# A quantised cross-attention with a gated LoRA layer: the order of four small products, and the queue of 32 stores

## The chip, the cores and the metric

The kernel runs on one core of one Trainium2 chip. A core has a tensor engine (PE; its weight loads are listed as PEld), a vector engine (DVE), a scalar engine (ACT), GpSimd (POOL) and SyncE (SP), which here only issues DMA transfers. The metric is the device time of one execution in microseconds, as the median of several runs.

## The reference

Two residual steps on x of shape 2 x 1024 x 2048, float32. The first adds a quantised product with a context of 2 x 2048 x 2048; the second adds a linear layer with one shared low-rank adapter and one that is a sum of sixteen, weighted by a gate. The 2 x 1024 rows form eight groups of 256, and each has its own row of the gate:

```python
q1 = fake_quant(_layernorm(x), x1_scale, x1_zp)     # clip(round(v / s + z), 0, 255), back to float
q2 = fake_quant(ctx_4096, x2_scale, x2_zp)
x = x + jnp.matmul(q1, q2)

h = _layernorm(x)
base_out = jnp.matmul(h, kernel) + bias
A_eff = jnp.einsum('bn,nri->bri', gate, lora_A)      # gate 8 x 16, lora_A 16 x 32 x 2048
B_eff = jnp.einsum('bn,nor->bor', gate, lora_B)      # lora_B 16 x 2048 x 32
h8 = h.reshape(8, 256, 2048)
Ax = jnp.einsum('bri,bti->btr', A_eff, h8)
delta = jnp.einsum('bor,btr->bto', B_eff, Ax)
delta = delta + jnp.einsum('or,btr->bto', lora_B_shared, jnp.einsum('ri,bti->btr', lora_A_shared, h8))
x = x + base_out + delta.reshape(x.shape)
```

## The kernel before

The function works through the two batches one after the other. All of it is written in a framework whose scheduler, before the kernel runs, puts the instructions of each engine into one fixed order; only the entry of batch 0 has an order written out by hand. Every engine takes its instructions in that order, and an instruction that waits holds up all that stand behind it on its engine. A `high_priority` block, and a change in the work around an instruction, move it in that order.

**Cross-attention.** For each batch, the product is cut into four blocks n of 512 columns and four groups g of 256 rows, each with two row tiles j. One pair (n, g) is `xattn_pair`: for each j, ACT fills PSUM with the row and column terms (`begin`, L526), PE adds 16 products in bf16 (tile pa, L530, 16 products of 128 x 512), then DVE adds both row tiles to x (`end`, L547) and takes statistics for the second layer norm (L551). The right operand comes from the context, which SP loads in 512 KB pieces into buffers of a pool called lit and ACT and DVE quantise.

**Gating.** The gated adapters are made by PE: for each batch four blocks of A and four blocks of B, each of 512 columns. For one such block `gated_sums` (L570) takes two loaded buffers of two halves each; each half, 128 x 512 (the sixteen adapters by eight of the 32 ranks), goes through one float32 product with a matrix of gate values (gmat) into 32 of the 128 rows of one PSUM bank (eight ranks for each of the batch's four groups; tile pg_a or pg_b, L576). So a block has four products, c = 0 to 3. Each buffer is given back after its two products, and the next load is issued by `load_next` (L204) on SP's queue, from one list `todo` that holds the context's pieces and the adapters' in the order of their use. `gated_copy` (L588) copies the bank to SBUF on DVE (L591, buffers of a pool q2b). A's blocks are turned by PE and placed into acat (L594 to L610). B's blocks go to a DRAM tensor bd: `lora_b_step` (L612) issues eight stores for each block, each of 16 rows of 512 float32, 32 KB, from SP (L617). From bd they come back as tiles bp (L680, loads of 64 rows), of which the first two of a batch are issued from POOL's queue and the others from ACT's.

**From cross-attention to the second layer.** When a group's 256 rows are finished, `group_z` normalises them: DVE works out the scale of each row tile from the statistics (L334 to L358) and scales it in two halves (z, L629), PE transposes each half in two sets (tile ptz, L633), ACT copies these to SBUF (L634), and ACT's queue stores the result to DRAM (zs, L640, four stores of 512 KB for each group). `lora_ax` multiplies two groups with acat (px, L649).

**Second layer.** The product with the weight is a Strassen-like scheme, twice nested. SP loads blocks of the weight of 1 MB (big<-in_w_dram, L753), DVE adds two of them (L763) into operands named b11, b12, b22, b21 and combines these (L772); POOL does the same for the operands made from z (a11, a21, a22, a12 and the sums s1, s2). PE multiplies (tiles fu, fv, fw, L829), DVE adds the results to y (L853), and the second adapter product (pl, L695) needs bp. The first operands of a batch, and first products fu, are prepared while its cross-attention still runs, and stand among its instructions.

Of the kernel before, what the change touches and what calls it, by code (L numbers as in the profile page):

```python
# [98 lines left out]
def tile_quant_xattn_then_lora_ffn(  # L99
# [17 lines left out]
    nc = tc.nc  # L117
# [15 lines left out]
    GP = GPB * RC  # L133
# [21 lines left out]
    gmat = const.tile([P, 2, GPB // 2, RC], F32, tag="gmat", name="gmat")  # L155
# [48 lines left out]
    def load_next():  # L204
        while todo and len(loaded) < ahead[0] and todo[0][0] <= batch[0] and lit.spare:
            _, srcs = todo.popleft()
            if isinstance(srcs, int):
                load_x(0, srcs)
                continue
            buf = lit.take()  # L210
            t = flat(buf).rearrange("p (k n) -> p k n", k=2)
            if len(srcs) == 1:
                nc.sync.dma_start(out=t, in_=srcs[0])
            else:
                for c, src in enumerate(srcs):
                    nc.sync.dma_start(out=t[:, c, :], in_=src)
            loaded.append((len(srcs), buf, t))

    def next_loaded(parts):

        got = next(e for e in loaded if e[0] == parts)
        loaded.remove(got)
        return got[1:]
# [342 lines left out]
    def gated(nm):  # L566

        return gated_copy(gated_sums(nm))

    def gated_sums(nm):  # L570
        ps = ps_m.tile([P, NB], F32, tag="pm", name=f"pg_{nm}")
        for h in range(2):
            buf, t = next_loaded(2)
            for c in range(2):
                row = (2 * h + c) * GP
                nc.tensor.matmul(  # L576
                    ps[row : row + GP, :],
                    gmat.rearrange("p i a r -> p (i a r)"),
                    t[:, c, :],
                    start=True,  # L580
                    stop=True,
                    skip_group_check=True,
                )
            lit.give(buf)
            load_next()
        return ps
# [25 lines left out]
    def lora_b_step(b, n):  # L612

        st, sf = gated(f"b{b}_{n}")
        for c in range(NC):
            for i in range(2):
                nc.sync.dma_start(  # L617
                    out=bd[b][i::2, i, ds(c * RC, RC), ds(n * NB, NB)],
                    in_=sf[ds(c * GP + i * (GP // 2), GP // 2), :],
                )  # L620
        q2b.give(st)
# [301 lines left out]
    def entry():  # L923
# [21 lines left out]
        def ad_sums(n):  # L945
            ad[n] = gated_sums(f"a0_{n}")
# [74 lines left out]
    for b in range(B):  # L1021
# [35 lines left out]
        for g in range(GPB):  # L1057
# [6 lines left out]
            if g == 2:  # L1064
                column_term(b, 3, c2[3])
        lora_b_step(b, 0)
        close_c2(2)
        bp.give(colt.pop(2))
# [3 lines left out]
        for g in range(GPB):  # L1072
            xattn_pair(b, 3, g, c1T, c2[3])
            big.give(c1T_bufs[g])
            if g == 0:
                first.block("b11")
                first.load("b12")
            elif g == 1:
                first.block("b12")
                first.comb("t1", "b12", "b11", ALU.subtract)  # L1080
            elif g == 2:
                first.load("b22")
            if g < 3:
                lora_b_step(b, g + 1)
            if g > 0:
                zqs[g - 1] = [lit.take() for _ in range(4)]
                group_z(b, g - 1, wk, zqs[g - 1])
            if g == 2:

                lora_ax(b, 0, [zqs[0], zqs[1]])  # L1090
                for i in range(2):
                    for j in range(2):
                        first.t[f"a{i + 1}{j + 1}"] = zqs[i][j]
                        lit.give(zqs[i][2 + j])
# [127 lines left out]
```

## Time and profile before

| what | value |
|---|---|
| median of three runs | 1090.15 us (1088.11 to 1092.04) |
| span of the profiled execution | 1086.6 us |
| PE busy | 1063.4 us in 3932 records |
| DVE busy | 759.3 us |
| POOL busy | 267.8 us |
| ACT busy | 247.6 us |
| granted clock of PE, mean | 0.994 |

The span runs from the first to the last instruction that the profiler saw in one execution; the time of a run also holds what lies around it, so it is some microseconds longer (3.5 us between this span and the median). Busy times are per engine, and engines work beside each other. In a row such as "L530 PE MATMUL pa<-big,big 128*128 128x512 bf16 x1024 | 238.8, 381 | 5.0 <-DVE big L428 2.6", the parts are: line, engine, operation, output and inputs, shape, number; then busy microseconds and the mean nanoseconds of one; then how long the engine sat idle just before such instructions and what ended most of that. A float32 product shows as two records. In timelines the columns are start, duration, engine, line, operation, tile, count, and in brackets an idle time ahead of it with what ended it. SPq and ACTq are the queues in which SP and ACT issue transfers.

### The profile page before, as it was taken

How to read it: one execution, taken by the hardware profiler on the slowest of the kernel's cores; microseconds unless marked ns; L12 is line 12 of the kernel's file. 1: busy time of each engine (PE TensorE's matmuls, PEld its weight loads, DVE VectorE, ACT ScalarE, POOL GpSimd, SP SyncE). 2: the span in 40 equal slices, each digit the busy share in tenths (PEclk: the TensorE clock that was granted, in tenths of full speed). 3: DMA queues.
4: the chain of work that ended last, by engine and by line, in shares of the span. 5: the costliest groups of instructions: out<-in, count | busy, mean ns of one | idle time of the engine just before them, and what ended most of it. 6: DMA issues, size and time to landing. Idle time of an engine off the chain costs nothing.

```text
span 1086.6 us, 10640 instructions
## 1 busy us (share of the span) xinstructions
PE 1063.4 (98%) x3932; PEld 491.3 (45%) x3932; DVE 759.3 (70%) x941; ACT 247.6 (23%) x351; POOL 267.8 (25%) x112
## 2 busy tenths in 40 slices
PE   5999999999999999999999999999999999999998
PEld 2444445544444444444444433555444444444443
DVE  7986776756877686677858645757569677756851
ACT  5866133210000000001676631331000000000000
POOL 0000003243434314362000000034344532253500
PEclk7999999999999999999999999999999999999999
DMA  9979758876897575798682394679668874748511
GB/s 344 378 200 295 214 189 327 311 250 218 290 361 271 181 269 182 255 357 300 221 281 49 124 245 164 222 273 349 237 237 292 293 266 154 270 144 301 212 40 58
DMA packets 120380, 261.35 MB, mean 241 GB/s; under 512 B 11400, under 2 KB 15624, under 8 KB 119304
## 3 DMA queue, kind: packets, MB, share of 16 engines
q1 hardware_dynamic: 99840, 219.24, 59.1%
q10 hardware_dynamic: 20168, 40.38, 10.9%
q0 software_dynamic: 320, 1.05, 0.3%
q8 instruction: 31, 0.51, 0.2%
q14 instruction: 21, 0.17, 0.1%
HBM read 224.99 MB, written 37.75 MB: 242 GB/s over the span
## 4 chain that ended last, share of the span: by engine, by line
PE 87%; DVE 5%; DMA 4%; ACT 2%; issue 1%; SPq 0%; ACTq 0%
PE fu L829 34%; PE fv L829 17%; PE pa L530 14%; PE fw L829 9%; DMA lit<-in_ctx_dram 3%; PE pl L695 3%; PE px L649 3%; PE ptz L633 2%; DMA y<-in_x_dram 1%; PE pg_b L576 1%; DVE st L383 1%; PE pg_a L576 1%; ACT big L412 1%; PE pt L423 1%; DVE big L629 1%
## 5 line engine op out<-in xcount | busy, mean ns | idle before, releaser
L829 PE MATMUL fu<-big,lit 128*128 128x512 f32 x896 | 395.3, 593 | 0.0
L829 PEld LDWEIGHTS fu<-big,lit 128*128 128x128 f32 x896 | 168.7, 190 | 206.2 <-issue 204.9
L530 PE MATMUL pa<-big,big 128*128 128x512 bf16 x1024 | 238.8, 381 | 5.0 <-DVE big L428 2.6
L829 PE MATMUL fv<-big,lit 128*128 128x512 f32 x448 | 197.9, 594 | 0.0
L772 POOL TENSOR_TENSOR lit<-lit,lit 128x1024 f32<-128x1024 f32 x56 | 164.2, 2940 | 116.4 <-PE fw L829 49.2
L763 POOL TENSOR_TENSOR lit<-lit,lit 128x1024 f32<-128x1024 f32 x40 | 100.2, 2508 | 289.1 <-DMA lit<-zs 257.7
L772 DVE TENSOR_TENSOR big<-big,big 128x2048 f32<-128x2048 f32 x56 | 159.6, 2853 | 5.9 <-PE ptz L633 5.3
L530 PEld LDWEIGHTS <-big 128*128 128x128 bf16 x1024 | 96.7, 98 | 136.5 <-issue 31.8
L853 DVE TENSOR_TENSOR y<-y,fu 128x1024 f32<-128x1024 f32 x92 | 108.6, 1215 | 50.7 <-PE fu L829 50.5
L829 PEld LDWEIGHTS fv<-big,lit 128*128 128x128 f32 x448 | 84.3, 190 | 105.0 <-issue 104.7
L853 DVE TENSOR_TENSOR y<-y,fv 128x1024 f32<-128x1024 f32 x48 | 56.8, 1218 | 89.4 <-PE fv L829 89.4
L458 ACT ACTIVATE q2b<-lit,sc,inv 128x1024 int16<-128x1024 f32 x64 | 76.3, 1232 | 161.8 <-DMA lit<-in_ctx_dram 126.1
L763 DVE TENSOR_TENSOR big<-big,big 128x2048 f32<-128x2048 f32 x40 | 104.2, 2604 | 11.8 <-DMA big<-in_w_dram 11.8
L829 PE MATMUL fw<-big,lit 128*128 128x512 f32 x224 | 99.6, 593 | 0.0
L680 POOL DMA_DIRECT2D bp<-bd x4 | 2.7, 664 | 376.8 <-DVE rstd_z L358 183.4
L684 ACT COPY pl<-bias 128x1024 f32<-128x1024 f32 x16 | 16.3, 1018 | 294.4 <-DVE y L706 281.4
L547 DVE SCALAR_TENSOR_TENSOR y<-pa,k_s,y 128x1024 f32<-128x1024 f32 x32 | 41.0, 1280 | 47.0 <-PE pa L530 46.8
L829 PEld LDWEIGHTS fw<-big,lit 128*128 128x128 f32 x224 | 41.8, 190 | 51.4 <-issue 50.2
L853 DVE TENSOR_TENSOR y<-y,fw 128x1024 f32<-128x1024 f32 x24 | 28.4, 1216 | 50.9 <-PE fw L829 50.9
L526 ACT ACTIVATE pa<-bp,r_s 128x512 f32<-128x512 f32 x58 | 39.0, 685 | 84.8 <-PE pa L530 54.8
L383 DVE BATCH_NORM_STATS2 st<-y 128x6 f32<-128x512 f32 x64 | 41.4, 680 | 5.4 <-DMA y<-in_x_dram 5.3
L551 DVE BATCH_NORM_STATS2 st<-y 128x6 f32<-128x512 f32 x64 | 40.1, 678 | 0.1
(92 smaller groups left out, 637.3 us busy)
## 6 DMA issues: line engine op xcount, KB each, us to landing
big<-in_w_dram SPq DMA_DIRECT2D x96, 1024.0 KB
lit<-zs SPq DMA_DIRECT2D x88, 512.0 KB
lit<-in_ctx_dram SPq DMA_DIRECT2D x64, 512.0 KB
out_dram<-y ACTq DMA_DIRECT2D x30, 512.0 KB
zs<-lit ACTq DMA_DIRECT2D x24, 512.0 KB
lit<-in_lora_a_dram SPq DMA_DIRECT2D x32, 256.0 KB
lit<-in_lora_bt_dram SPq DMA_DIRECT2D x32, 256.0 KB
y<-in_x_dram SPq DMA_DIRECT2D x16, 512.0 KB
```

The source lines that it names most:

```text
L383: nc.vector.bn_stats(st1[:, self.m, n, :], self.y[:, ds(n * NB, NB)])
L458: nc.scalar.activation(qi, t, AF.Relu, bias=z2, scale=inv2)
L526: nc.scalar.activation(self.pa[:, j, :], colt[self.n], AF.Identity, bias=r_s[:, m : m + 1])
L530: nc.tensor.matmul(self.pa[:, j, :], self.c1T[:, k, ds(j * P, P)], self.c2[k // 8][:, k % 8, :], start=not self.begun[j], stop=(k == KT - ...
L547: return nc.vector.scalar_tensor_tensor(yp, self.pa, s12, yp, ALU.mult, ALU.add)
L551: nc.vector.bn_stats(st2[:, self.g * MG + j, self.n, :], y[self.g][:, j, ds(self.n * NB, NB)])
L649: nc.tensor.matmul(px[i * 2 * R : (i + 1) * 2 * R, :], acat[:, k, ds(3 * pr + i, 2), :].rearrange("p s r -> p (s r)"), zqs[i][k // KQ][:, ...
L695: nc.tensor.matmul(pl[j][i][:, half], axT[rows, pr, ds(j * P, P)], bt[rows, half], start=False, stop=True, skip_group_check=True,)
L763: line(eng.tensor_tensor(got[0], got[0], got[1], ALU.add if terms[1][2] > 0 else ALU.subtract))
L772: line(eng.tensor_tensor(out_t, at[p], at[q], op))
L829: nc.tensor.matmul(ps[m], at[:, k, ds(m * P, P)], bt[:, k, :], start=(opens and k == 0), stop=(ends and k == KQ - 1), skip_group_check=True,)
L853: line(nc.vector.tensor_tensor(yp, yp, whole[chain], op))
```

## The change

`gated_sums` takes both loaded buffers first, issues its four products one after the other in the order c = 3, 2, 1, 0, and gives both buffers back after the fourth, with the two next loads issued then. `lora_b_step` issues its eight stores on GpSimd's queue in place of SP's. Nothing else is edited; the lines after L577 move up by one.

```diff
     def gated_sums(nm):
         ps = ps_m.tile([P, NB], F32, tag="pm", name=f"pg_{nm}")
-        for h in range(2):
-            buf, t = next_loaded(2)
-            for c in range(2):
-                row = (2 * h + c) * GP
-                nc.tensor.matmul(
-                    ps[row : row + GP, :],
-                    gmat.rearrange("p i a r -> p (i a r)"),
-                    t[:, c, :],
-                    start=True,
-                    stop=True,
-                    skip_group_check=True,
-                )
+        got = [next_loaded(2) for _ in range(2)]
+        for c in (3, 2, 1, 0):
+            nc.tensor.matmul(
+                ps[c * GP : (c + 1) * GP, :],
+                gmat.rearrange("p i a r -> p (i a r)"),
+                got[c // 2][1][:, c % 2, :],
+                start=True,
+                stop=True,
+                skip_group_check=True,
+            )
+        for buf, _ in got:
             lit.give(buf)
             load_next()
         return ps
...
         for c in range(NC):
             for i in range(2):
-                nc.sync.dma_start(
+                nc.gpsimd.dma_start(
                     out=bd[b][i::2, i, ds(c * RC, RC), ds(n * NB, NB)],
                     in_=sf[ds(c * GP + i * (GP // 2), GP // 2), :],
                 )
         q2b.give(st)
```

## Prediction

> **What bounds the kernel now.** I read the page's head and busy times first, then the summary of the chain of waits, then the groups by line of the two gating products, and last the timelines of the engines in the stretches that the change touches (80 to 215 us for batch 0, 605 to 745 us for batch 1).
>
> ```profile
> span 1086.6 us, 10640 instructions
> PE 1063.4 (98%) x3932; PEld 491.3 (45%) x3932; DVE 759.3 (70%) x941; ACT 247.6 (23%) x351; POOL 267.8 (25%) x112
> PE 87%; DVE 5%; DMA 4%; ACT 2%; issue 1%; SPq 0%; ACTq 0%
> ```
>
> PE is the bound: 1063.4 of 1086.6 us busy, so at most 23 us could be won by filling its gaps, and most of those lie at the two ends. A microsecond of work taken from PE's row is a microsecond won, as long as nothing else is late. The groups by line, with shapes apart, give the touched products:
>
> ```profile
> L576 PE MATMUL pg_b<-lit,gmat 128*32 128x512 f32 x64 | 13.7, 605 | 0.0
> L576 PE MATMUL pg_a<-lit,gmat 128*32 128x512 f32 x64 | 12.7, 605 | 0.0
> ```
>
> 128 records are 64 products (two each), 16 blocks of four. The busy times differ though the counts agree; the chain in order of time (start, duration, what) tells why:
>
> ```profile
> 128.31 1.00 PE pg_b L576 x8
> 129.30 3.56 PE pa L530 x16
> 132.86 0.98 PE pg_b L576 x2
> 133.84 3.56 PE pa L530 x16
> 137.40 0.99 PE pg_b L576 x6
> ...
> 158.70 0.99 PE pg_b L576 x8
> ```
>
> Four products that stand together hold PE for 1.00 us, three for 0.99, one alone for 0.98: each uses 32 of PE's columns, and by these times neighbours run beside each other. A block that is split in 1 + 3 by 16 products of the cross-attention (pa, 3.56 us) costs 0.98 + 0.99 where a whole one costs 1.00.
>
> **The change part by part.** *One row.* Of 16 blocks, 9 are split so in this trace: three in batch 0 (starts at 104.87, 132.86, 141.95) and six in batch 1 (608.89, 636.99, 646.51, 657.97, 667.05, 676.14). In the order of instructions that the compiler gives the changed kernel all 16 stand as four in a row, at the place of the former lone one. That removes 9 x 0.98 = 8.8 us of PE work, 2.9 in batch 0 and 5.9 in batch 1. Taking both buffers at once adds a wait for the second load, but the adapter loads land early: the closest, pg_a of block 2, has its data at about 95.7 us for a use at 104.8, and those of B stand 20 us ahead. I cost it at nothing. That c runs 3 to 0 costs nothing either: same four, same columns. If the second load came late, the price would be that delay, once.
>
> *The stores.* 32 per batch leave SP's queue for POOL's. On SP they stand between the loads of the weight blocks:
>
> ```profile
> 126.61 2.10 SPq L753 DMA_DIRECT2D big<-in_w_dram  x2
> 130.25 5.24 SPq L617 DMA_DIRECT2D bd<-q2b  x8
> 137.43 0.93 SPq L753 DMA_DIRECT2D big<-in_w_dram  x2
> 139.34 18.47 SPq L617 DMA_DIRECT2D bd<-q2b  x16
> 157.92 1.37 SPq L753 DMA_DIRECT2D big<-in_w_dram  x2
> 160.65 10.68 SPq L617 DMA_DIRECT2D bd<-q2b  x8
> ```
>
> Eight take 5.2 us there. POOL has nothing between 2 us and 162.87 and issues only two loads of the same buffer (bp<-bd) before its first sum:
>
> ```profile
> 162.87 1.01 POOL L680 DMA_DIRECT2D bp<-bd  x1 [160.87 <-DMA zs<-lit]
> 180.60 0.54 POOL L680 DMA_DIRECT2D bp<-bd  x1 [16.71 <-DVE big L629]
> 181.16 9.50 POOL L772 TENSOR_TENSOR lit<-lit,lit 128x1024 f32<-128x1024 f32 x3
> ```
>
> The four issues of this kind in the whole trace take 538 to 1013 ns and their data lands in 5.2 to 6.0 us. No store is issued from POOL in this trace, so 0.54 and 1.01 us are the bounds from the nearest rows: 17 to 32 us per batch, in at least 50 us of an idle engine (130.5, the first copy of B, to 181). What queues behind them there are the bp loads, first needed by PE at 199.1 us (pl, L695), and the sums s1, s2, needed by PE at about 208.5. Both have 15 us or more left, so I cost the issues at nothing; without that cover 32 x 0.66 us, the four rows' mean, would be 21 us a batch. The ninth store and later ones wait for a lane that an earlier store frees, and the copy of the fourth B block waits for the first eight stores; at 6 us to landing these are done long before.
>
> The row that speaks against it is the 1013 ns issue, which stands beside the scaling of z on DVE (L629), where those beside other work of DVE took 0.54 to 0.56 us. The Trainium skill ("SBUF — State Buffer", section "SBUF: two separate sides") says that GpSimd writes the descriptors itself and is kept from it while DVE holds the port they share, 620 ns alone and 3100 beside a DVE copy; by that figure 32 stores would be an estimated 99 us a batch at the worst, and the sum would turn to a loss.
>
> *What moves on DVE.* This is the costly side. Without stores before them, SP's weight loads are expected earlier, and the compiler places DVE's weight sums (L763) earlier in DVE's order too: b12 now ahead of the end of pa_3_1 (L547) and of z_1 (L629), b22 ahead of the statistics and z_2, b21 ahead of z_5. PE's transposes ptz wait for z. DVE takes its queue in order, so each of these is a wait for a load with z behind it. In the old order:
>
> ```profile
> 146.52 1.28 DVE L547 SCALAR_TENSOR_TENSOR y<-pa,k_s,y 128x1024 f32<-128x1024 f32 x1 [3.00 <-PE pa L530]
> ...
> 149.51 2.27 DVE L763 TENSOR_TENSOR big<-big,big 128x2048 f32<-128x2048 f32 x1
> 151.70 0.81 DVE L629 TENSOR_SCALAR big<-y,mv_z,rstd_z 128x1024 f32<-128x1024 f32 x1
> ...
> 169.50 2.29 DVE L763 TENSOR_TENSOR big<-big,big 128x2048 f32<-128x2048 f32 x1 [1.01 <-DMA big<-in_w_dram]
> ```
>
> b12: its loads can issue at about 136.4 (pg's old 137.40 less the lone 0.98); those issued at 126.61 and 128.34 let DVE begin at 135.00, 8.4 to 8.9 us after the first. So L763 runs 145.3 to 147.5, then L547 (+1.2), L772 (+2.2), two statistics (+1.2), z_1 first half (+0.75): 152.85, where PE wants it at 151.84 in the shortened row. 1.05 us in batch 0 (0.3 to 1.9 as the load lands 0.75 earlier or 0.85 later), and with batch 1's rows 0.75 (0.3 to 2.35).
>
> b22: its loads issue when pa_3_2 leaves PE (158.7 before). Alone a pair is seen by DVE about 5.5 us after its last issue slot frees, beside the 2 MB of z stores up to 7.0; then L763 2.25, small operations 0.9, first half of z_2 0.75: 9.4 to 10.9 us. PE has 8.9 us between: pg 0.99, 12 pa 2.67, 2 fu 1.72, 16 pa 3.56. Stall 0.5 to 2.0, I take 1.25, in each batch 2.5 together. After that the transposes go at ACT's pace of 1.33 us per eight instead of 1.09 between pa products used up earlier: about 0.24 in each batch, 0.5 (0 to 1). New waits: 1.05 + 0.75 + 2.5 + 0.5 = 4.8 us.
>
> *What is given back.* Transposes stall in the old order too: the gaps at 184 and 719 (0.5 and 0.8 us before ptz of z_5, whose half takes 2.43 and 2.66 us beside POOL's sums instead of 0.81), and unfilled transposes at 165 to 169. In the new order z_5 stands behind b21's sum and the transposes behind fu products, so I count half of the gaps, 0.6, and 0.7 for the transposes of z_2 and z_3 (eight times 1.33 against 1.24 with fillers): 1.3 us (0 to 2.6, twice that).
>
> Sum: -8.8 + 4.8 - 1.3 = -5.3 us. The profiled execution had 1086.6 us of span; the three runs' median is 1090.15, 3.5 us above, of which the start and end around the span are a part. I subtract from the median: 1084.9 us. The bounds together: -8.8 + 1.6 - 2.6 = -9.8, and -8.8 + 9.3 - 0 = +0.5, so 1080.4 to 1090.6.
>
> **The rivals.** *The whole gain arrives.* If the weight loads, freed of the stores, land before DVE reaches them, the 4.8 us of new waits shrink to 0.5: 1090.15 - 8.8 - 0.5 = about 1080.9 us. For it: the SP queue above, where 16 stores stood between two loads. Against it: a load begins only when its buffer comes free, which PE's row sets, not SP.
>
> *The waits eat it.* At the upper bounds (1.9 + 2.35 + 2.0 + 2.0 + 1.0 = 9.3 us) nothing is left: 1087 with half of that excess over the 4.8 (-5.3 + 2.2), 1090.6 with all of it and nothing given back. For it: DVE operations stretch threefold beside POOL's sums (0.81 to 2.43), and a weight load beside z stores needed 11 us (157.92 to 169.02). Against: those sums begin only at 181.
>
> *Slower: POOL's queue is late.* One mechanism: each store holds POOL for more than 2.0 us, because it is issued beside busy DVE. From 130.5 to the need of s1 and s2 at 208.5 less 9.5 us of sums there are 68.5 us for 34 issues, 2.0 each; in batch 1 (658.5 to 744, less 9.5) 76 us, 2.2. At 2.3 us the delay is 34 x 0.3 = 10 and 34 x 0.1 = 3.4 us, which gives 1084.9 + 13.6 = 1098.5; 3 us each gives over 1130. For it: the 1.01 us row. Against: it is half the deciding price, and DVE is idle for 17.6 of the 50.5 us from 130.5 to 181.
>
> *It does not do what it says.* The row stays split or its gain shifts to the next load (batch 1's pa wait for ctx loads around 621 to 631): 2 to 4 us less won, 1087 to 1089, counted with the second rival.
>
> **How the numbers follow.** Forecast 0.44; whole gain 0.20; waits eat it or shift 0.26; POOL late 0.10. Three microseconds (0.3%) is about what a measurement of this kernel can tell from no change, so faster is below 1086.9 and slower above 1093.4. Of the forecast's own range 0.42 of 0.44 and the whole gain's 0.20 fall below, with some of the eaten case (0.02): faster 0.64. Same: 0.24 + 0.02 = 0.26. Slower 0.10. For 8 in 10 the range runs from 1080.0, a little under the whole gain, to 1090.6, where the eaten case ends; it leaves out POOL late and the tails.
>
> **What would show it.** Right: the gating groups' busy time falls from 13.7 + 12.7 = 26.4 us to about 26.4 - 8.8 = 17.6, PE's busy time down by 8 to 9 us, and new PE idle before ptz of z_1 and z_2 with DVE L763 as releaser after a wait for in_w. Wrong: no such idle (first rival), 2 us or more each (second), POOL's bp issue past 185 with PE waiting at pl or fu (third). The prediction is wrong in its base if PE's busy time does not fall.

## The result, and the profile after

The changed kernel takes 1104.45 us in the median (1103.79 to 1107.81) where the kernel before took 1089.13 us beside it: a ratio of 1.0143, 95% interval 1.0118 to 1.0168. It is slower by 15 us; the forecast was 5 us faster. The head of its page, and the summary of its chain:

```profile
span 1106.0 us, 10666 instructions
...
PE 1062.2 (96%) x3932; PEld 495.7 (45%) x3932; DVE 757.1 (68%) x941; ACT 247.2 (22%) x351; POOL 300.1 (27%) x176
...
PE 75%; DVE 11%; DMA 9%; ACT 3%; issue 2%; SPq 0%; ACTq 0%; DVEq 0%
```

The span grew by 19.4 us, more than the 15 of the medians: the execution profiled is the slowest of the four (1107.81 us). PE is idle for 1106.0 - 1062.2 = 43.8 us where it was idle for 23.2, and its busy time fell by only 1.2 us. DVE and DMA now hold 20% of the chain where they held 9%. The groups of the gating products, shapes apart, show that the edit itself did what it says:

```profile
L574 PE MATMUL pg_b<-lit,gmat 128*32 128x512 f32 x64 | 8.5, 605 | 0.0
L574 PE MATMUL pg_a<-lit,gmat 128*32 128x512 f32 x64 | 8.5, 605 | 0.0
```

26.4 us became 17.0. What PE waited for in the changed kernel (microseconds in total, times, longest), next to 1.3 and 1.2 us for the same two rows before:

```profile
PE ptz L632 <- DVE big L628: 15.6, 7, 6.5
...
PE pa L530 <- ACT pa L526: 6.8, 7, 2.0
```

The transposes wait for z. The chain in order of time (start, duration, what) follows the first long one of these waits back:

```profile
163.82 0.66 PE pa L530 x3
164.49 0.02 issue
164.50 7.67 DMA big<-in_w_dram
172.17 0.02 issue
172.20 2.29 DVE big L762
...
175.33 0.73 DVE big L628
176.06 0.04 issue
176.11 1.97 PE ptz L632 x8
```

The loads of weight block b22 begin when the last product of pa_3_2 has left PE, land 7.7 us later; DVE sums them (L762) and only then scales z_2 (L628). Scaling z_2 does not need the weight at all; it stands behind the sum in DVE's order. The same view in batch 1, for b21 and z_5:

```profile
718.43 8.98 DMA big<-in_w_dram
727.41 0.02 issue
727.44 2.29 DVE big L762
729.73 0.13 DVE r_z L347 x2
729.86 2.22 DVE nt_z L349 x2
732.09 0.19 DVE nt_z L350 x2
732.27 2.17 DVE rstd_z L358 x2
734.44 2.77 DVE big L628
737.21 0.14 issue
737.35 1.94 PE ptz L632 x8
```

9 us of load, 2.3 of sum, and then DVE's small operations, some of them at 2.2 us a pair where a pair took 0.35 before z_2 (at 710.27): POOL's sums had begun beside them at 727.96. And the eight transposes take 1.94 us, not 1.06. The windows of that stretch (window, length, busy time of PE, PEld, DVE, ACT and POOL, then PE's granted clock, share of DMA, GB/s) tell why:

```profile
737.30:738.30 1.00, 0.95 (x5) 0.98 (x6) 0.63 (x1) 0.00 (x0) 0.00 (x0) 0.50 0.00 0
738.30:739.30 1.00, 1.00 (x6) 1.00 (x5) 0.00 (x0) 0.59 (x1) 0.00 (x0) 0.50 0.00 0
739.30:740.30 1.00, 1.00 (x2) 0.34 (x2) 0.81 (x1) 0.59 (x1) 0.00 (x0) 0.50 0.15 61
740.30:741.30 1.00, 1.00 (x4) 0.51 (x3) 0.00 (x0) 0.00 (x0) 0.00 (x0) 0.50 1.02 418
741.30:742.30 1.00, 1.00 (x7) 1.00 (x6) 0.00 (x0) 0.42 (x1) 0.00 (x0) 0.58 0.51 115
742.30:743.30 1.00, 1.00 (x5) 0.52 (x4) 0.77 (x1) 0.76 (x2) 0.00 (x0) 1.00 0.85 303
```

After the wait PE runs at half its clock, for about 4.8 us here, 2.9 us after the wait that ends at 176.11 and 3.0 us after a third that ends at 711.88. I estimate that half of these 10.7 us, 5.3 us, is lost so. The gating products gave back 9.4 us and PE's busy time fell by 1.2; the clock is 5.3 of the 8.2 between them.

GpSimd's queue, on the other hand, is as quiet as was forecast. Its timeline in batch 0:

```profile
134.81 4.61 POOL L616 DMA_DIRECT2D bd<-q2b  x8 [132.81 <-ACT pa L526]
140.09 4.44 POOL L616 DMA_DIRECT2D bd<-q2b  x8 [0.68 <-DMA bd<-q2b]
...
174.61 0.58 POOL L679 DMA_DIRECT2D bp<-bd  x1 [3.45 <-DMA bd<-q2b]
190.97 7.57 POOL L771 TENSOR_TENSOR lit<-lit,lit 128x1024 f32<-128x1024 f32 x3 [15.78 <-PE px L648]
```

All 64 issues take 562 to 712 ns, and POOL then waits 15.8 us for PE before its first sum.

### The profile page after: what moved, and what is told of

The parts are those of the page before. It is cut to its first block, busy times and chain, and to the rows that moved or that the text cites. A ratio compares the mean times of both kernels' runs of the same rounds, so it can differ in the third digit from the quotient of the medians.

```text
span 1106.0 us, 10666 instructions
## 1 busy us (share of the span) xinstructions
PE 1062.2 (96%) x3932; PEld 495.7 (45%) x3932; DVE 757.1 (68%) x941; ACT 247.2 (22%) x351; POOL 300.1 (27%) x176
## 4 chain that ended last, share of the span: by engine, by line
PE 75%; DVE 11%; DMA 9%; ACT 3%; issue 2%; SPq 0%; ACTq 0%; DVEq 0%
PE fu L828 34%; PE fv L828 17%; PE fw L828 9%; PE pa L530 6%; DMA big<-in_w_dram 5%; PE pl L694 3%; PE ptz L632 2%; PE px L648 2%; DMA lit<-in_lora_a_dram 2%; DVE st L551 2%; DVE st L383 2%; DVE big L762 1%; DVE y L547 1%; DMA lit<-in_ctx_dram 1%; DVE big L628 1%
## 5 line engine op out<-in xcount | busy, mean ns | idle before, releaser
L771 POOL TENSOR_TENSOR lit<-lit,lit 128x1024 f32<-128x1024 f32 x56 | 161.4, 2891 | 155.4 <-PE fw L828 63.9
L762 POOL TENSOR_TENSOR lit<-lit,lit 128x1024 f32<-128x1024 f32 x40 | 99.8, 2496 | 295.1 <-DMA lit<-zs 253.9
L771 DVE TENSOR_TENSOR big<-big,big 128x2048 f32<-128x2048 f32 x56 | 156.7, 2802 | 5.1 <-PE ptz L632 4.5
L616 POOL DMA_DIRECT2D bd<-q2b x64 | 35.8, 567 | 305.4 <-ACT pa L526 273.4
L762 DVE TENSOR_TENSOR big<-big,big 128x2048 f32<-128x2048 f32 x40 | 101.8, 2545 | 24.5 <-DMA big<-in_w_dram 24.5
L458 ACT ACTIVATE q2b<-lit,sc,inv 128x1024 int16<-128x1024 f32 x64 | 76.1, 1231 | 165.1 <-DMA lit<-in_ctx_dram 144.7
L547 DVE SCALAR_TENSOR_TENSOR y<-pa,k_s,y 128x1024 f32<-128x1024 f32 x32 | 41.0, 1280 | 26.4 <-PE pa L530 26.3
L526 ACT ACTIVATE pa<-bp,r_s 128x512 f32<-128x512 f32 x58 | 38.9, 684 | 87.6 <-PE pa L530 56.3
L632 PE MATMUL ptz<-ident,big 128*128 128x128 f32 x256 | 38.3, 297 | 15.7 <-DVE big L628 15.6
L628 DVE TENSOR_SCALAR big<-y,mv_z,rstd_z 128x1024 f32<-128x1024 f32 x32 | 31.7, 1009 | 25.3 <-PE ptz L632 25.2
```

Of the source, the lines that this page charges most:

```text
L458: nc.scalar.activation(qi, t, AF.Relu, bias=z2, scale=inv2)
L526: nc.scalar.activation(self.pa[:, j, :], colt[self.n], AF.Identity, bias=r_s[:, m : m + 1])
L547: return nc.vector.scalar_tensor_tensor(yp, self.pa, s12, yp, ALU.mult, ALU.add)
L616: nc.gpsimd.dma_start(out=bd[b][i::2, i, ds(c * RC, RC), ds(n * NB, NB)], in_=sf[ds(c * GP + i * (GP // 2), GP // 2), :],)
L628: nc.vector.tensor_scalar(t, y[g][:, m % MG, ds(h * H, H)], mean, rstd, ALU.subtract, ALU.mult)
L632: nc.tensor.transpose(pt[:, k, :], t[:, ds((4 * u + k) * P, P)], ident)
```

## The experiments

**Theory O** (order): moving the stores off SyncE changes where the scheduler puts the weight sums in DVE's queue, ahead of z, and PE waits for z behind a load; the row of four products does the same on a small scale on ACT. **Rival Q**: GpSimd's queue, or its kind of transfer, makes loads or issues late. **Rival R**: holding both buffers until the fourth product makes the next loads late. Medians below stand beside the kernel before on the same chip; since that base differs by up to 2 us from chip to chip, gains are compared through it.

**The row alone**: the changed kernel with its stores back on SyncE.

```diff
-                nc.gpsimd.dma_start(
+                nc.sync.dma_start(
```

> The four products in one row, the stores left on SyncE. In the order of DVE's instructions the weight sums b12 and b22 then stand behind the end of pa_3_1 and behind z_2, as before the change. Theory O (the early place of the weight sums in DVE's queue makes the loss): about 1089 - 8.8 = 1080, up to 1084 with small waits. Rival R (holding both buffers until the fourth product makes the next loads late): 1095 or more, with the wait of 1.95 us of PE for the row terms (L526) near 104 us still there. Rival Q (GpSimd's queue itself is the cost): the same as O, so this run tells R from the others.

Measured: 1085.79 us beside 1088.04, ratio 0.9982 (0.9960 to 1.0003). Nearly nothing of the 8.8 us arrives. PE's busy time fell to 1056.4 us, but its waits show one new row, and one that has grown from 1.2 us:

```profile
PE fw L828 <- DVE big L762: 3.6, 2, 2.1
PE pa L530 <- ACT pa L526: 3.3, 5, 1.2
```

So R is not the 15 us, but its wait near 104 us is there (2.65 us in the three pieces between 100 and 126), smaller than R said.

**The stores alone**: the kernel before with GpSimd's queue.

```diff
-                nc.sync.dma_start(
+                nc.gpsimd.dma_start(
```

> The stores on GpSimd, the gating products as before the change (split in 1 + 3). DVE's order has the weight sums b12 and b22 early, as in the changed kernel. Theory O: about 15 + 8.8 us slower than before, 1105 to 1113, with PE's idle time before the transposes ptz ended by DVE's scaling of z. Rival Q: the same time, but with late issues or late loads of bp on POOL. Rival R: 1086 to 1092, as before.

Measured: 1112.16 us beside 1088.04, ratio 1.0226 (1.0213 to 1.0239). The waits:

```profile
PE ptz L633 <- DVE big L629: 15.9, 5, 5.5
```

The whole loss comes with this half of the change, and PE waits for DVE, as in the changed kernel. It does not yet tell O from Q.

**The order put back**: the changed kernel, all stores on GpSimd, with three ties (`issue_after` puts an instruction behind the named one in the order).

```diff
-            xattn_pair(b, 3, g, c1T, c2[3])
+            summed = xattn_pair(b, 3, g, c1T, c2[3])
...
+                with tc.issue_after(summed.ins):
+                    first.block("b12")
...
+        with tc.issue_after(z_of[4, 0].ins):
+            first.block("b22")
...
+        with tc.issue_after(z_of[5, 1].ins):
+            first.block("b21")
```

> The changed kernel, stores on GpSimd and products in one row, but the three weight sums of the first operands are tied behind the end of pa_3_1, behind the first half of z_4 and behind z_5 on DVE, which is their order before the change. Theory O: the waits before ptz and their slow clock go; 1079 to 1087 us. Rival Q (GpSimd's queue or its transfers): still 1098 or more, since all 64 stores are still issued there. Rival R: still 1095 or more.

Measured: 1088.47 us beside 1088.04, ratio 1.0006 (0.9993 to 1.0019). Of the 15.3 us over the base 0.4 are left though all 64 stores are still issued from GpSimd; the waits before ptz fall from 15.6 to 1.1 us. That refutes Q as the main cause of the loss. It does not show that the queue costs nothing: the row with its stores on SyncE, 1085.79 beside the same base, is 2.7 us faster. The time is 1.5 us above the range that O gave: L526's waits are still there.

```profile
PE pa L530 <- ACT pa L526: 5.2, 7, 1.6
...
PE fw L830 <- DVE big L764: 1.5, 1, 1.5
PE ptz L634 <- DVE big L630: 1.1, 2, 0.8
```

**Another queue**: the changed kernel with the stores on ACT (nc.scalar in place of nc.gpsimd).

> The changed kernel with the stores on ACT's queue in place of GpSimd's. The order of DVE's instructions has the weight sums still earlier, b12 ahead of z_0 and b21 ahead of the second half of z_3. Theory O: slow though GpSimd issues nothing, 1100 us or more. Rival Q: 1080 to 1090, since GpSimd is free.

Measured: 1110.71 us beside 1088.04, ratio 1.0207 (1.0194 to 1.0220). GpSimd issues no store here and the loss is larger. ACT itself is late too (9.2 us of waits for L526), so this run alone would not show O, but it contradicts Q.

**The early order without the change**: the kernel before, both edits left out, b12's sum put ahead of pa_3_1's end and b22's ahead of z_2.

```diff
+            with tc.issue_after(sums["b12"]) if (self.n, self.g) == (3, 1) else nullcontext():
                 return nc.vector.scalar_tensor_tensor(yp, self.pa, s12, yp, ALU.mult, ALU.add)
...
+            with tc.issue_after(sums["b22"]) if (m, h) == (2, 0) else nullcontext():
                 nc.vector.tensor_scalar(t, y[g][:, m % MG, ds(h * H, H)], mean, rstd, ALU.subtract, ALU.mult)
...
+            if g == 1:
+                first.block("b12")
+                sums["b12"] = line.last
             xattn_pair(b, 3, g, c1T, c2[3])
...
                 first.load("b22")
+                first.block("b22")
+                sums["b22"] = line.last
```

> The kernel before, with stores on SyncE and split gating products, but with the weight sum b12 ahead of the end of pa_3_1 and b22's ahead of z_2 on DVE; the scheduler then puts b21's ahead of z_5 by itself. Neither edit of the change is in it. Theory O (the place of the sums in DVE's order makes the loss): 8 to 22 us slower than before, 1096 to 1110, with PE's waits before ptz of z_2 ended by DVE's scaling of z and a clock of 0.5 after the longer ones. Rival Q or R (queue or row): 1086 to 1091, as before.

Measured: 1097.61 us beside 1089.68, ratio 1.0070 (1.0055 to 1.0085), 7.9 us. The order, with stores on SyncE, makes a loss of this kind: the wait before z_2 is 0.70 us in batch 0 and 2.31 us in batch 1, with a clock of 0.50 after it. It is at the low end, and a third of the 24.1 us that the stores alone cost, which is the run to compare with, since neither has the row's gain. The place of the sums on DVE is not the whole of it, then: PE's order differs too. Between the start of b22's loads in batch 0 and the transposes of z_2 PE has 13.0 us of work here, seven fu products among it, and 8.8 us with three in the run with the stores alone. So it waits 0.70 us here and 5.00 there, though the load took 10.5 us here and 9.9 there. And b21's sum, done at 183.1 and 722.2, holds up no z_5. No run takes PE's order by itself.

**One sum at a time**: the changed kernel with one of the three ties.

```diff
+        with tc.issue_after(z_of[4, 0].ins):
+            first.block("b22")
```

> The changed kernel with only b22's sum tied, behind the first half of z_4; b12's sum stays early. The order then has b21's sum of batch 1 behind z_5 too. Theory O with the clock: PE's waits of 2.78 and 3.49 us before ptz of z_2 go with the 2.9 us of slow clock after them, and the 6.45 us of batch 1 with 2.2 us behind it: 15 to 18 us, 1087 to 1092. Without the clock's share: 12 us, 1092 to 1094.

Measured: 1093.23 us beside 1087.87, ratio 1.0047 (1.0034 to 1.0060): 10.0 us less over its base than the changed kernel. The time is inside what O gave without the clock's share (1092 to 1094), and the gain is below both of its figures. Part of the reason is in the trace: a wait of 3.96 us appeared at a later transpose of batch 0 (190.78), behind b21's sum, with 3 us at a clock of 0.50 after it.

```diff
+        with tc.issue_after(z_of[5, 1].ins):
+            first.block("b21")
```

> The changed kernel with only b21's sum tied, behind z_5; b12's and b22's stay early. Theory O with the clock: 6.45 and about 1 us of waits and 2.2 us of slow clock go, 9 to 10 us, 1094 to 1097; without the clock's share about 7, 1097 to 1099. The waits of 2.8 and 3.5 us before ptz of z_2 stay.

Measured: 1105.30 us beside 1087.87, ratio 1.0152 (1.0134 to 1.0170). A miss: nothing is won. The waits before z_2 stay (2.84 and 2.92 us), as expected. The 6.45 us before z_5 went, but another wait stands in their place. DVE's timeline in batch 1, and PE's:

```profile
733.23 4.45 DVE L764 TENSOR_TENSOR big<-big,big 128x2048 f32<-128x2048 f32 x1
```

```profile
737.73 3.06 PE L830 MATMUL fw<-big,lit 128*128 128x512 f32 x4 [2.84 <-DVE big L764]
```

The sum now runs beside POOL's sums (729.96 to 739.87) and takes 4.45 us instead of 2.29, and fw needs it; after the wait PE has 3.4 us at a clock of 0.50. A wait of 2.61 us at 594.90 (0.51 in the changed kernel) is in this execution too, and I have no cause for it. So tying b21 alone wins nothing. In the order before, the rest of pa_3_3 and most fu products stood after the transposes of z_2; where b22's sum is early, PE has used them up by then, and I read the miss so, though no run took this alone.

**ACT's order put back**, without and with the stores on GpSimd (the second also has the three ties):

```diff
+            begins[self.n, self.g, j] = ins.ins
...
+                with tc.issue_after(begins[2, 1, 0]) if (b, r) == (0, 6) else nullcontext():
+                    quantise(c2[3], r)
```

> The products in one row with the stores on SyncE, and one rounding of the context on ACT (L458, the seventh piece of block 3 in batch 0) tied behind the first begin of pa_2_1 (L526), as it stood before the change. Theory O (each loss is a place in an engine's queue behind a load): PE's three waits for L526 between 100 and 126 us, 1.24 + 0.63 + 0.78 = 2.65 us, go, and the time falls by 2 to 3 us from the run with the row alone, to about 1083. Rival (the loads themselves are later when both buffers are held): no change, 1085 to 1087.

> The changed kernel, stores on GpSimd, with the weight sums tied as in the run before and the rounding on ACT tied too. Theory O: 2 to 3 us below 1088.5, about 1086. Rival: no change from 1088.5.

Measured: 1083.24 us beside 1087.87, ratio 0.9964 (0.9943 to 0.9985); and 1085.62, ratio 0.9978 (0.9965 to 0.9990). Both as O said: 2.4 and 2.7 us over their bases from one instruction's place, with both buffers still held; the second is clear of the noise, of the first (12 runs against 11, overlapping) the size is less sure. That settles R's wait near 104 us. ACT's order with the row alone, and before:

```profile
99.50 2.37 ACT L458 ACTIVATE q2b<-lit,sc,inv 128x1024 int16<-128x1024 f32 x2 [2.92 <-DMA lit<-in_ctx_dram]
101.77 1.28 ACT L526 ACTIVATE pa<-bp,r_s 128x512 f32<-128x512 f32 x2
```

```profile
99.15 1.28 ACT L526 ACTIVATE pa<-bp,r_s 128x512 f32<-128x512 f32 x2
100.38 3.49 ACT L458 ACTIVATE q2b<-lit,sc,inv 128x1024 int16<-128x1024 f32 x3
```

It was not a late load but a rounding (L458) that stood ahead of two begins (L526) and waited for a load; SyncE issued the last two of these loads at 91.40, and at 91.45 before the change.

**Only the last eight stores moved**: the row, ACT's tie, and GpSimd's queue for the fourth block of B alone.

```diff
-                nc.sync.dma_start(
+                (nc.gpsimd if n == 3 else nc.sync).dma_start(
```

> The products in one row, the rounding on ACT tied as before, and only the last eight stores of a batch, which stand on SyncE between the loads of b22 and b21, on GpSimd's queue; the other 24 stay on SyncE. DVE's order keeps the sums late without any tie. Theory O: PE's wait for b21's sum before fw, about 2 us a batch with the row alone, shrinks: 1079 to 1082 us. Rival (that wait comes from the load's own start, when pa_3_3 is done, and not from the stores): 1083, as with the rounding tied and all stores on SyncE.

Measured: 1080.38 us beside 1089.68, ratio 0.9912 (0.9898 to 0.9926), better than both kernels by clear margins. PE's waits at fw are gone. DVE's two sums of b22 and b21 in batch 0, here:

```profile
168.51 2.29 DVE L765 TENSOR_TENSOR big<-big,big 128x2048 f32<-128x2048 f32 x1 [2.39 <-DMA big<-in_w_dram]
...
182.32 2.29 DVE L765 TENSOR_TENSOR big<-big,big 128x2048 f32<-128x2048 f32 x1
```

and with the row alone:

```profile
170.58 2.29 DVE L762 TENSOR_TENSOR big<-big,big 128x2048 f32<-128x2048 f32 x1 [1.22 <-DMA big<-in_w_dram]
...
186.32 3.65 DVE L762 TENSOR_TENSOR big<-big,big 128x2048 f32<-128x2048 f32 x1 [2.94 <-DMA big<-in_w_dram]
```

The first load of b21 is issued at 170.84, as soon as b22's sum (to 170.80) frees its buffer; with the row alone at 174.37, 1.5 us after that sum, with the eight stores on SyncE until 172.36. The second is issued in both when pa_3_3 leaves PE (175.74 and 178.98), as the rival said; but DVE then has b21's sum done 8.9 us later instead of 11.0, with 1.4 us of the difference in the sum itself and the rest in the load. The sum itself no longer stands beside POOL's sums, which run from 173.60 to 181.16 here and from 183.04 to 192.18 with the row alone. And DVE's order stayed late without a tie. Why the load is shorter was not tried apart.

## Why the prediction was wrong

The step that failed is the price of what moves on DVE. The prediction gave 4.8 us of new waits less 1.3 given back; the changed kernel shows 18.4 us of waits in these places where the kernel before had 1.3. On top come two terms that the prediction left out: 3.4 us of waits on ACT and about 5.3 of slow clock.

*One row, 8.8 us.* Right in kind and size: 26.4 us of busy time became 17.0, 9.4 by that row. The kernel with the last eight stores moved is 9.3 us under its base, what the rival "whole gain arrives" gave; it needs ACT's tie for that.

*The stores.* Right that they cost nothing on POOL: 562 to 712 ns each against bounds of 538 and 1013. The price quoted from the Trainium skill ("SBUF — State Buffer", section "SBUF: two separate sides"), 3100 ns beside a DVE copy, did not appear in any of the 64 issues. The page means a copy from SBUF to SBUF, and DVE's copy of the second B block (137.88), which falls among them, reads PSUM, so no run here tests that price. The rival on the slow side was wrong too: the kernel is slower, and POOL's queue is idle.

*What moves on DVE.* This step failed, though it had named the mechanism. "Alone a pair is seen by DVE about 5.5 us after its last issue slot frees, beside the 2 MB of z stores up to 7.0": the loads took 7.67 and 8.22 us. No row of the kernel before shows 5.5: its six sums that waited for a load began 6.7 to 10.6 us after the later of the two issues (178.54 to 186.07 for b21, 7.5). So the waits at z_2 were 2.78 and 3.49 us, above the 2.0 that I gave as the upper end; the second rival had waits of 2 us or more as its sign, but its price ended at 9.3 us. For b12 the waits were 1.45 + 1.51 = 2.96 us in batch 0 and 1.35 + 0.31 = 1.66 in batch 1, where I took 1.05 and 0.75; only batch 1 is inside its bounds.

*What is given back.* Wrong in sign. I counted b21's earlier place as a gain of 0.6 us. It put a load that can only begin when pa_3_3 is done ahead of z_5: a wait of 6.45 us in batch 1, with DVE's operations stretched beside POOL's sums. In batch 0 the sum was done at 186.88, in time; PE's 1.04 us before z_5 there come from the stretch alone (POOL's sums 190.97 to 198.54), as the 0.52 before the change did. The forecast had that stretch in a row (0.81 to 2.43) and used it only for the rival, with the reason against it that "those sums begin only at 181"; with z_5 late, they were side by side.

*Left out: the clock.* I priced each wait at its own length. Waits of 2.78, 3.49 and 6.45 us were followed by 10.7 us at half clock, 5.3 us more; one of 1.95 us at 104 was not. The Trainium skill ("TensorE: Matmul & The Clock Gate", section "Part 1: The HAM clock gate") puts such a drop after one idle window of about 3.4 us, and the return after as much work. The return is near the 2.9 and 3.0 us after two of the waits and not the 4.8 after the third; for the drop, 2.78 us of idle time was already enough.

*Left out: ACT.* 1.95 + 0.63 + 0.78 = 3.36 us before the change even reaches B. I had compared the orders on PE and DVE closely, not that of ACT's roundings.

The sum as it came out: -8.8, ACT 3.4, b12 4.6, b22 6.3, before z_5 7.5 less the old 1.3, clock 5.3: +17.0 of the 19.4 us of span. About 2.4 us are not assigned; PE's idle time is accounted for (20.5 of the 20.6 us by which it grew), so they lie in its busy time. The clock's share is read from the windows; no run took it away by itself.

Not settled: the 2.9 us (4.7 through their bases) between the row with ACT's tie and the version that moves the last eight stores; and whether GpSimd's queue keeps a cost once the order is put back, 2.7 us without ACT's tie and 2.4 with it, the latter not clear of the noise. The single execution profiled of the row with ACT's tie took 1090.15 us, longer than its median of 1083.24, so its waits at fw (4.68 and 2.82 us) are not typical of it.

## What to carry to other kernels

When a scheduler orders in-order queues, moving transfers from one queue to another can change the order of engines that the diff does not mention, here most likely because it then expects other loads earlier: read the new order on every engine, and price each instruction that now waits for a load by everything queued behind it. A load whose start is set by the bound engine (a buffer that comes free) does not come earlier by emptying its queue. The three long waits on PE cost about 1.4 times their length by the estimate above, and in these runs the cure was a few ties, or moving only those transfers that really stand before a load that is needed.

## What the runs showed of the hardware

PE's clock fell to 0.50 after waits of 2.78 us and more in the changed kernel, but not always: with the stores on ACT's queue one wait of 2.21 us (until 160.0) was followed by a clock of 0.50 half a microsecond later and another of 2.21 us (until 700.9) by none; with b21 tied alone, waits of 2.84 and 2.92 us were followed by full clock in the one case and by 0.50 about 1.5 us after work had begun again in the other. A wait of 2.31 us in the early order without the change was followed by 0.50 as well. So in these runs the length alone does not decide between 2.2 and 2.9 us; waits of 3.49 us and more were followed by it each time that I looked.
